# Another split of the first weight's load, and expert results collected at four points per unit, in a one-core MoE residual kernel

## The chip, the core and the metric

The kernel runs on one core of one Trainium2 chip. The metric is device time in microseconds (us), the median of the runs. All data are float32.

## What is computed

```python
x = x + L0(x, cond)      # L0: ys = cond / sqrt(512)
                         #     d  = rsqrt((ys*ys) @ (W*W) + 1e-8)
                         #     L0 = ((x * ys) @ W) * d        (per batch row)
x = x + L1(x, cond)      # L1: shared = (silu(xf @ w1) * (xf @ w3)) @ w2
                         #     s = sigmoid([xf, cond] @ router_W); top 2 of s + bias
                         #     routed = sum of 2 gates * (gelu(xf @ W1e[e]) @ W2e[e])
                         #     L1 = (shared + routed) / 3
```

x is 4 x 1024 x 512 (4096 tokens), W is 512 x 512, w1 and w3 are 512 x 1024, and there are 8 experts with 512 hidden features each.

## The kernel before, in words

The 4096 tokens are eight blocks of 512. The work has four stages, and each engine's instructions are issued in the order in which the program writes them.

**Front (L0, lines 191 to 491).** W is the tile `w0t`, 128 partitions by four chunks k of 512 columns; the product of a block sums over the four chunks. `load_w0` (L188) loads chunk by chunk: one DMA for each k, four of 256 KB, from SP's queue, behind the small load of `cond` (L191). From ACT's queue the first half of block 0 of x is loaded (L178, four DMAs, one per quarter g of 32 partitions). While these come, TensorE runs five matmuls on zeros (`WARM`, L203) and then turns `cond` (four transposes, L233), from which VectorE makes the scales `ysT` (L234, L235) and their squares (L237). Then, for each chunk k: VectorE scales the chunk into `wm` (`modulate`, L266) and turns a quarter of x (`turn_x`, L278), and ACT squares the chunk (`w0sq`, L285). On ACT's queue, behind the square of chunk 1 and of chunk 2, two loads each of the second half of block 0 are issued, and behind the square of chunk 3 the four loads of block 1. TensorE runs the products of block 0's first half chunk by chunk (L439, 16 products of 256 columns), then the norms (L313), then the second half with the rest of the norm inside (L326, L331). VectorE turns block 1 of x *before* it works out the norm (L338 to L346) and the residual sums of block 0 (L350). Block 1's products need the PSUM banks that those sums read. SP loads block 3 as soon as block 0's buffer is free.

**Shared experts, six blocks**, then **34 slots of 256 gathered tokens each** plus a number of further slots that a `Switch` takes from the data (`Slot`, weights fetched per slot, results `yr` written to DRAM as `ys_d`, L873).

**Tail: the shared experts of the last two blocks**, eight units (`Shared`, L673), called U0 to U7 below, four per block. A unit does two hidden chunks by one level of Strassen's method. On TensorE its order is: product 1 and product 2 (`begin`), products 6 and 7 in turn, product 5, the output product of the unit before (`second(0)`, L774), product 3, `second(1)`, product 4. Products 1, 6, 5, 3 go to two `ch` banks, products 2, 7, 4 to two `ot` banks (all four banks of the pool, so the next unit needs the same ones). ACT copies partial sums out of `ch` (L730) and does the SiLU (L754, L755, L764). VectorE adds `ot` to them (L734, three pairs: `add(LO, 0, LO)`, `add(HI, 1, HI)`, `add(HI, 1, LO)`) and multiplies (L756, L757 for the first chunk, L765 for the second). The last pair, `add(HI, 1, LO)`, follows product 4, and the next unit's product 2 cannot start before it, since it writes the same banks.

Beside this the tail collects the routed results, token tile by token tile (32 tiles of 128 tokens). `gather_picks(t)` fetches the tile's row from DRAM (SP, L668), copies two address columns (VectorE, L890) and issues two indirect DMAs of 256 KB from `ys_d` (GpSimd, L891) into one of ten places. `add_picks(t)` adds both with their gates (VectorE, L901, two instructions) and, for the 24 tiles of the first six blocks, writes the tile out (SP, L903). The eight tiles of the last two blocks are held until their own block's sum is added (L787) and written (L791).

When this happens is set by the list `tasks` (L941 to L977): two points per unit, one behind L757 (`task(2 * self.at)`, L758) and one behind L765 (L766). The 32 tiles are spread over 12 of the 16 points, the held eight first; a tile is added two points after its gather. Two other jobs sit in this list: `turn_last` (L922, four transposes, in U1 behind L757) and `token_sums` (L403, in U2 behind L765). Four instructions L787 lie in U4 between L757 and `add(HI, 1, LO)`.

Of the kernel before, what the change touches and what calls it, by code (L numbers as in the profile page):

```python
# [32 lines left out]
P = 128  # L33
Q = 32
# [5 lines left out]
TAIL = 2  # L40
WARM = 5
# [3 lines left out]
def kernel(  # L45
# [14 lines left out]
    nc = tc.nc  # L60
    B, S, D = x.shape
    HS = w1.shape[1]
    E, _, HE = w1e.shape
    N = B * S
    KC = D // P
    NB = N // TB
    NS = TB // P
    NT = N // P
# [11 lines left out]
    early = NB - TAIL  # L80
# [17 lines left out]
    def bank_b(name):  # L98
        return ps_b.tile([P, TB], FP, tag="b", name=name)
# [58 lines left out]
    w0_sb = w0t.rearrange("p (k d) -> p k d", k=KC)  # L158
# [12 lines left out]
    HU, KH, TH = HSC // 2, KC // 2, TB // 2  # L171

    def new_seg(blk):
        segs[blk] = seg3[:, ts((blk + 1) % 3, SEG)].rearrange("p (q c) -> p q c", c=P)

    def load_segments_part(eng, blk, lo, n, g):
        v = x_f[ds(blk * TB + lo, n)].rearrange("(q i) (g c) -> g i q c", i=Q, c=P)
        eng.dma_start(out=segs[blk][ts(g, Q), ds(lo // Q, n // Q)], in_=v[g])  # L178
# [3 lines left out]
        for g in range(KC):  # L182
            load_segments_part(eng, blk, 0, TB, g)

    def load_w0(eng, k):

        v = w0.rearrange("(g k j) o -> k g j o", g=KC, k=KC)
        eng.dma_start(out=w0_sb[:, k, :], in_=v[k])  # L188


    nc.sync.dma_start(out=cond_sb, in_=cond)  # L191
    new_seg(0)
    for k in range(KC):
        load_w0(nc.sync, k)
    for g in range(KC):
        load_segments_part(nc.scalar, 0, 0, HALF, g)


    idle = x1T6[:, 0, :]
    nc.vector.memset(idle, 0.0)  # L200
    pz = bank_b("pz")
    for _ in range(WARM):
        nc.tensor.matmul(pz, lhsT=idle[:, :P], rhs=idle, start=True, stop=True)  # L203
    nc.scalar.activation(newt, idle[:, : KC * B], AF.Square)

# [2 lines left out]
        out=ident4, in_=ident4, compare_op=ALU.not_equal, fill=1.0, base=0, pattern=[[-1, B]], channel_multiplier=1  # L208
# [4 lines left out]
    for k in range(KC):  # L213
        nc.gpsimd.affine_select(
            out=fold[ts(k, Q)],
            in_=fold[ts(k, Q)],
# [14 lines left out]
    pc = bank_b("pc")  # L231
    for k in range(KC):
        nc.tensor.transpose(pc[:, ds(k * B, B)], cond_p[:, k], ident4)  # L233
    nc.vector.tensor_copy(condT, pc[:, : KC * B].rearrange("p (k b) -> p k b", b=B))  # L234
    nc.vector.tensor_scalar(ysT, condT, scale, None, ALU.mult)  # L235
    nc.vector.memset(ys2, 0.0)
# [6 lines left out]
        out=before, in_=before, compare_op=ALU.is_ge, fill=1.0, base=0, pattern=[[-1, P]], channel_multiplier=1  # L243
# [154 lines left out]
    def token_sums(blk):  # L398
        b = x1T[blk]
        k1, k2 = slice(0, KH), slice(KH, KC)  # L400
        v = t_tiles[blk % 2].rearrange("p (n k t) -> p n k t", n=3, k=KH)
        t1, t2, t4 = (v[:, n] for n in range(3))
        sub = lambda o, i0, i1: nc.vector.tensor_tensor(o, i0, i1, ALU.subtract)  # L403
        sub(t1, b[:, k1, HI], b[:, k1, LO])
        sub(t2, b[:, k2, HI], t1)
        sub(b[:, k1, HI], b[:, k2, HI], b[:, k1, HI])
        sub(t4, b[:, k2, LO], t2)
        t_of[blk] = (t1, t2, b[:, k1, HI], t4)
# [252 lines left out]
    def segment_index(lo, hi):  # L661
        nc.vector.tensor_scalar(toks[:, lo:hi], later["toks_raw"][:, lo:hi], float(KC), part, ALU.mult, ALU.add)

    held = {}

    def fetch_row(t, rows_d):
        held[t] = row_tile(f"row{t}")
        nc.sync.dma_start(out=held[t], in_=rows_d[ts(t, P)])  # L668
# [4 lines left out]
    class Shared:  # L673
# [62 lines left out]
        def rest(self, prev, task):  # L736
            g, h = self.c = [t.rearrange("p (m t) -> p m t", m=2) for t in (later["g"], later["h"][self.at % 2])]
            self.h = h
            self.evict(0, LO)
            for i in range(2):  # L740
                self.product(self.chain[i][:, LO], i, 6, False)
                if not self.seven:
                    self.product(self.other[i][:, HI], i, 7, True)
            self.add(LO, 0, LO)
            self.evict(1, LO)
            for i in range(2):
                self.product(self.chain[i][:, LO], i, 5, False)
            self.evict(1, HI)
            if prev is not None:
                prev.second(0)  # L750
            self.add(HI, 1, HI)
            for i in range(2):
                self.product(self.chain[i][:, LO], i, 3, False)
            nc.scalar.activation(g[:, 0, HI], self.chain[0][:, LO], AF.Silu)  # L754
            nc.scalar.activation(g[:, 0, LO], g[:, 0, LO], AF.Silu)  # L755
            nc.vector.tensor_tensor(h[:, 0, HI], g[:, 0, HI], self.chain[1][:, LO], ALU.mult)  # L756
            nc.vector.tensor_tensor(h[:, 0, LO], g[:, 0, LO], h[:, 0, LO], ALU.mult)  # L757
            task(2 * self.at)  # L758
            if prev is not None:
                prev.second(1)  # L760
            for i in range(2):
                self.product(self.other[i][:, HI], i, 4, False)
            self.add(HI, 1, LO)
            nc.scalar.activation(g[:, 1, :], g[:, 1, :], AF.Silu)  # L764
            nc.vector.tensor_tensor(h[:, 1, :], g[:, 1, :], h[:, 1, :], ALU.mult)  # L765
            task(2 * self.at + 1)  # L766

        def second(self, m):
            blk, u = self.blk, self.u
            hc = 2 * u + m  # L770
            if hc == 0:
                self.py[blk] = [bank_b(f"ps{blk}_{s}") for s in range(NS)]
            for s in range(NS):
                nc.tensor.matmul(  # L774
                    self.py[blk][s],
                    lhsT=self.h[:, m, ts(s, P)],
                    rhs=w2_sb[:, hc, :],
                    start=(hc == 0),
                    stop=(hc == HSC - 1),
                )  # L780
            if blk < early and HSC - 1 > hc >= HSC - 1 - NS:
                fetch_row(blk * NS + hc - (HSC - 1 - NS), x1_d)
            if hc == HSC - 1:
                for s in range(NS):
                    t = blk * NS + s
                    r = held.pop(t)
                    nc.vector.scalar_tensor_tensor(r, self.py[blk][s], third, r, ALU.mult, ALU.add)  # L787
                    if blk < early:
                        nc.scalar.dma_start(out=base_d[ts(t, P)], in_=r)
                    else:  # L790
                        nc.sync.dma_start(out=out_f[ts(t, P)], in_=r)  # L791
# [90 lines left out]
    def gather_picks(t):  # L882

        fetch_row(t, base_d if t < early * NS else x1_d)
        spot = len(order) % 10 * 2
        order.append(t)
        picks[t] = [big[1 + (spot + i) // KC][:, (spot + i) % KC, :] for i in range(2)]
        for i in range(2):
            at = later["addr"][i][:, t : t + 1]
            nc.vector.tensor_copy(at, idx[i][:, t : t + 1])  # L890
            nc.gpsimd.indirect_dma_start(  # L891
                out=picks[t][i],
                out_offset=None,
                in_=ys_d,
                in_offset=bass.IndirectOffsetOnAxis(ap=at.bitcast(U32), axis=0),
                bounds_check=ROWS - 1,
            )

    def add_picks(t):
        for i, y in enumerate(picks.pop(t)):  # L900
            nc.vector.scalar_tensor_tensor(held[t], y, gate[i][:, t : t + 1], held[t], ALU.mult, ALU.add)  # L901
        if t < early * NS:
            nc.sync.dma_start(out=out_f[ts(t, P)], in_=held.pop(t))  # L903
# [22 lines left out]
    late = len(units)  # L926
# [4 lines left out]
    tasks = {i: [] for i in range(2 * len(units))}  # L931
# [37 lines left out]
        tasks[7 + i].append(lambda i=i: scatter(2 * i, 2))  # L969
    for blk in range(1, early):  # L970
        tasks[2 * blk * HU - 3].append(lambda blk=blk: token_sums(blk))
    span = 2 * TAIL * HU - 4
    mine = [early * NS + i for i in range(TAIL * NS)] + list(range(early * NS))
    for i, t in enumerate(mine):
        u = 2 * late + i * span // len(mine)
        tasks[u].append(lambda t=t: gather_picks(t))
        tasks[u + 2].append(lambda t=t: add_picks(t))  # L977

    for s in range(NS):
        fold_logits(NB - 2, s)  # L980
# [7 lines left out]
    for u, unit in enumerate(units):  # L988
        if u == late:
            for n in tc.Switch(later["spare"], E):  # L990
                prev.end = SURE + n
                last = prev
                for j in range(SURE, SURE + n):
                    slot = Slot(j)
                    slot.at, slot.end = prev.at + 1 + j - SURE, SURE + n
                    slot.begin()
                    slot.rest(last, lambda i: None)
                    last = slot
                last.second(0)
                last.second(1)  # L1000
            prev = None
        if u > 0:
            unit.begin()
        if u == late:
            unit.sevens()
        unit.rest(prev, run_tasks)
        prev = unit
# [41 lines left out]
```

## Time and profile before

| | |
|---|---|
| median of 3 runs | 1243.74 us (1243.33 to 1243.89) |
| the profiled execution | 1241.12 us, its span 1239.3 us |
| TensorE matmul busy | 1217.4 us (98%), mean granted clock 0.997 |
| VectorE, ACT, GpSimd busy | 414.6 us, 172.7 us, 425.3 us |
| first product of x (L439) | 12.35 us from the span's start |
| first product of block 1 | 33.90 us |
| tail, U0 to U7 and the last sums | from 1074 us to the end |
| one undisturbed unit of the tail | 18.95 us |

Times inside the profiled execution count from the start of its span.

### The profile page before, as it was taken

To read this page: it belongs to the slowest core of one execution; us is meant where nothing else is said; L and a number is where in the kernel's file an instruction comes from. 1 tells how busy PE (TensorE), PEld (TensorE's weight loads), DVE (VectorE), ACT (ScalarE), POOL (GpSimd) and SP (SyncE) were. 2 spreads that over 40 slices of the span, in tenths; PEclk is the share of its full clock that TensorE was granted. 3 is DMA by queue.
4 is the path that set the end of the run, shared out by engine and by line. 5 is a ranking of instruction groups with operands and counts; after the bars stand their busy time and mean duration, and the time that the engine had idled before them with its cause. 6 is when DMAs were issued, how large, how long until landed. Compare 5 with 4: busy or idle time off the path is not lost.

```text
span 1239.3 us, 13133 instructions
## 1 busy us (share of the span) xinstructions
PE 1217.4 (98%) x4394; PEld 818.3 (66%) x4394; DVE 414.6 (33%) x958; ACT 172.7 (14%) x379; POOL 425.3 (34%) x448
## 2 busy tenths in 40 slices
PE   8999999999999999999999999999999999989998
PEld 5444576777767767767666666666666666667665
DVE  3537565422232332222212211221122121146763
ACT  1000031211111112112100000000000000111111
POOL 3000000343430121202465566556655660046550
PEclk9999999999999999999999999999999999999999
DMA  6599413201103041310488888888878885356881
GB/s 133 107 224 218 93 35 92 53 0 35 35 1 107 26 155 58 85 51 18 126 206 220 228 230 232 217 234 235 232 216 233 236 224 170 128 179 188 292 309 68
DMA packets 120894, 183.80 MB, mean 148 GB/s; under 512 B 15060, under 2 KB 50004, under 8 KB 120808
## 3 DMA queue, kind: packets, MB, share of 16 engines
q1 hardware_dynamic: 82696, 116.58, 35.5%
q0 software_dynamic: 16448, 35.26, 11.0%
q10 hardware_dynamic: 21664, 30.94, 7.8%
q8 instruction: 38, 0.62, 0.3%
q14 instruction: 48, 0.39, 0.2%
HBM read 138.09 MB, written 44.64 MB: 147 GB/s over the span
## 4 chain that ended last, share of the span: by engine, by line
PE 92%; DMA 3%; DVE 2%; issue 1%; another core or an unknown queue 0%; SPq 0%; ACTq 0%; ACT 0%; DVEq 0%
PE ph L844 18%; PE py L868 18%; PE ch L703 17%; PE ps L774 17%; PE ot L703 13%; PE pl L439 8%; DMA w0t<-in_L_cond_weight_dram 1%; PE pq L368 1%; DMA big<-in_L_cond_W1e_dram 1%; DMA seg<-in_x_dram 1%; DVE row L901 0%; DMA ys_d<-yr 0%; PE pr L384 0%; DMA xsegs<-x_d 0%
## 5 line engine op out<-in xcount | busy, mean ns | idle before, releaser
L814 POOL DMA_INDIRECT xsegs<-x_d,toks x280 | 285.1, 1018 | 367.2 <-issue 128.1
L868 PE MATMUL py<-big,h 128*128 128x512 f32 x544 | 238.8, 592 | 0.0
L774 PE MATMUL ps<-w_sb,h 128*128 128x512 f32 x512 | 229.8, 592 | 0.0
L868 PEld LDWEIGHTS py<-big,h 128*128 128x128 f32 x544 | 103.4, 190 | 116.0 <-issue 114.3
L872 DVE COPY yr<-py 128x512 f32<-128x512 f32 x68 | 46.9, 691 | 367.4 <-issue 207.9
L644 POOL DMA_INDIRECT tok_d<-token,addr x64 | 63.5, 992 | 294.3 <-DVE addr L634 276.0
L774 PEld LDWEIGHTS ps<-w_sb,h 128*128 128x128 f32 x512 | 97.3, 190 | 96.0 <-issue 92.6
L439 PE MATMUL pl<-xT,wm 128*128 128x512 f32 (+1 forms) x288 | 118.8, 561 | 5.9 <-DVE xT L278 4.6
L844 PE MATMUL ph<-xg,big 128*128 128x256 f32 x544 | 120.3, 379 | 1.1 <-DMA big<-in_L_cond_W1e_dram 1.1
L844 PE MATMUL ph<-t,big 128*128 128x256 f32 x544 | 120.2, 379 | 0.0
L844 PEld LDWEIGHTS ph<-xg,big 128*128 128x128 f32 x544 | 103.3, 190 | 22.3 <-issue 9.1
L844 PEld LDWEIGHTS ph<-t,big 128*128 128x128 f32 x544 | 103.4, 190 | 21.3 <-issue 8.1
L703 PE MATMUL ot<-big,w_sb 128*128 128x256 f32 x448 | 110.4, 379 | 1.4 <-DVE row L787 1.4
L891 POOL DMA_INDIRECT big<-ys_d,addr x64 | 67.3, 1052 | 111.8 <-DMA row<-x_d 63.4
L851 ACT ACTIVATE h<-ph 128x512 f32<-128x512 f32 x68 | 40.6, 597 | 421.3 <-PE ph L844 252.2
L703 PEld LDWEIGHTS ot<-big,w_sb 128*128 128x128 f32 x448 | 85.0, 190 | 14.1 <-DVE row L787 1.8
L734 DVE TENSOR_TENSOR g<-ot,g 128x256 f32<-128x256 f32 x96 | 40.6, 423 | 155.0 <-PE ot L703 103.9
L439 PEld LDWEIGHTS pl<-xT,wm 128*128 128x128 f32 x288 | 53.5, 194 | 57.4 <-issue 46.3
L703 PE MATMUL ch<-w0t,seg 128*128 128x256 f32 x256 | 62.7, 380 | 2.6 <-issue 2.5
L703 PE MATMUL ch<-t,seg 128*128 128x256 f32 x256 | 63.1, 379 | 0.0
L734 DVE TENSOR_TENSOR h<-ot,h 128x256 f32<-128x256 f32 x96 | 40.6, 423 | 62.1 <-PE ot L703 39.0
L756 DVE TENSOR_TENSOR h<-g,ch 128x256 f32<-128x256 f32 x32 | 13.5, 421 | 134.5 <-PE ch L703 109.4
(163 smaller groups left out, 945.6 us busy)
## 6 DMA issues: line engine op xcount, KB each, us to landing
big<-in_L_cond_W1e_dram SPq DMA_DIRECT2D x136, 256.0 KB
big<-in_L_cond_W2e_dram SPq DMA_DIRECT2D x34, 1024.0 KB
ys_d<-yr ACTq DMA_DIRECT2D x68, 256.0 KB
x_d<-back SPq DMA_DIRECT2D x32, 256.0 KB
row<-x_d SPq DMA_DIRECT2D x32, 256.0 KB
out_dram<-row SPq DMA_DIRECT2D x32, 256.0 KB
base_d<-row ACTq DMA_DIRECT2D x24, 256.0 KB
row<-base_d SPq DMA_DIRECT2D x24, 256.0 KB
```

Of the source, the lines that this page charges most:

```text
L439: nc.tensor.matmul(pas[oc][:, ds(lo, n)], lhsT=wms[b][:, k, oc, :], rhs=xTs[blk][:, k, ds(lo, n)], start=(k == 0), stop=(k == KC - 1),)
L644: ins = nc.gpsimd.indirect_dma_start(out=tok_d, out_offset=bass.IndirectOffsetOnAxis(ap=later["addr"][i][:, t : t + 1].bitcast(U32), axis= ...
L703: nc.tensor.matmul(out, lhsT=lhs[:, k, :], rhs=rhs[:, k, :], start=start and k == 0, stop=k == KH - 1, skip_group_check=not start,)
L734: nc.vector.tensor_tensor(c[:, m, cols], p[:, half], c[:, m, cols], ALU.add)
L756: nc.vector.tensor_tensor(h[:, 0, HI], g[:, 0, HI], self.chain[1][:, LO], ALU.mult)
L774: nc.tensor.matmul(self.py[blk][s], lhsT=self.h[:, m, ts(s, P)], rhs=w2_sb[:, hc, :], start=(hc == 0), stop=(hc == HSC - 1),)
L814: nc.gpsimd.indirect_dma_start(out=seg[:, q, :], out_offset=None, in_=x1_segs, in_offset=bass.IndirectOffsetOnAxis(ap=toks[:, c : c + 1].b ...
L844: nc.tensor.matmul(ph[:, i], lhsT=weights[j][0][:, k, ts(hp * per + i, P)], rhs=xg[j][:, k, :], start=(k == 0), stop=(k == KC - 1),)
L851: nc.scalar.activation(self.h[:, ts(hp, per), :], ph, AF.Gelu)
L868: nc.tensor.matmul(py, lhsT=self.h[:, hc, ts(s, P)], rhs=weights[j][1][:, hc, :], start=(hc == 0), stop=(hc == HC - 1))
L872: nc.vector.tensor_copy(r, py)
L891: nc.gpsimd.indirect_dma_start(out=picks[t][i], out_offset=None, in_=ys_d, in_offset=bass.IndirectOffsetOnAxis(ap=at.bitcast(U32), axis=0) ...
```

## The change

Two places are edited.

In the front, W comes in eight DMAs instead of four: first chunk 0 alone, in four parts of 32 partitions (64 KB each), then, for each quarter of 32 partitions, its chunks 1 to 3 in one DMA (192 KB each). All are still issued from SP. The second batch stands behind the loads of x in the program, which go through ACT's queue. Of the five matmuls on zeros, two stay ahead of the transposes of `cond`, and three run behind them.

In the tail, a list `pumps` with a counter `passed` replaces `tasks` for the picks. `pump()` is called four times per unit: behind `add(LO, 0, LO)` (point 0), behind `add(HI, 1, HI)` (point 1), behind L757 and the unit's first task (point 2), and at the end behind its second task (point 3): 32 points in all. Tile i of the list is gathered at point 25 i / 32, rounded down, and added six points later, ahead of that point's gathers. The list is in another order: the four tiles of block 6, twelve early ones, the four of block 7, the other twelve. `turn_last`, `reload_last` and `token_sums` stay in `tasks`.

```diff
-    def load_w0(eng, k):
-        v = w0.rearrange("(g k j) o -> k g j o", g=KC, k=KC)
-        eng.dma_start(out=w0_sb[:, k, :], in_=v[k])
+    def load_w0(eng, g, lo, hi):
+        v = w0.rearrange("(g k j) o -> g j k o", g=KC, k=KC)
+        eng.dma_start(out=w0_sb[ts(g, Q), lo:hi, :], in_=v[g][:, lo:hi, :])
...
-    for k in range(KC):
-        load_w0(nc.sync, k)
+    for g in range(KC):
+        load_w0(nc.sync, g, 0, 1)
     for g in range(KC):
         load_segments_part(nc.scalar, 0, 0, HALF, g)
+    for g in range(KC):
+        load_w0(nc.sync, g, 1, KC)
...
-    for _ in range(WARM):
+    for _ in range(WARM // 2):
         nc.tensor.matmul(pz, lhsT=idle[:, :P], rhs=idle, start=True, stop=True)
...
     for k in range(KC):
         nc.tensor.transpose(pc[:, ds(k * B, B)], cond_p[:, k], ident4)
+    for _ in range(WARM - WARM // 2):
+        nc.tensor.matmul(pz, lhsT=idle[:, :P], rhs=idle, start=True, stop=True)
...
+    pumps, passed = {}, []
+    def pump():
+        if not passed:
+            return
+        for work in pumps.get(passed[0], []):
+            work()
+        passed[0] += 1
...
             self.add(LO, 0, LO)
+            pump()
...
             self.add(HI, 1, HI)
+            pump()
...
             task(2 * self.at)
+            pump()
...
             task(2 * self.at + 1)
+            pump()
...
-    span = 2 * TAIL * HU - 4
-    mine = [early * NS + i for i in range(TAIL * NS)] + list(range(early * NS))
+    mine = list(range(early * NS))
+    mine = [early * NS + i for i in range(NS)] + mine[: len(mine) // 2] + list(range(NT - NS, NT)) + mine[len(mine) // 2 :]
+    points = 4 * TAIL * HU
     for i, t in enumerate(mine):
-        u = 2 * late + i * span // len(mine)
-        tasks[u].append(lambda t=t: gather_picks(t))
-        tasks[u + 2].append(lambda t=t: add_picks(t))
+        p = i * (points - 7) // len(mine)
+        pumps.setdefault(p, []).append(lambda t=t: gather_picks(t))
+        pumps.setdefault(p + 6, []).insert(0, lambda t=t: add_picks(t))
...
         if u == late:
+            passed.append(0)
             unit.sevens()
```

## Prediction

> **What bounds the kernel now.** I read the page's first part, the chain of work for the front, a table of 1 us stretches of the front, the waits of TensorE, and the timeline of the tail. The page says that only TensorE matters:
>
> ```profile
> PE 1217.4 (98%) x4394; PEld 818.3 (66%) x4394; DVE 414.6 (33%) x958; ACT 172.7 (14%) x379; POOL 425.3 (34%) x448
> ```
>
> So the change is worth what it takes from the stretches in which TensorE waits. The chain of the first 45 us (start, length, what) shows the first of them:
>
> ```profile
> 3.09 16.73 DMA w0t<-in_L_cond_weight_dram
> ...
> 19.84 0.33 ACT w0sq L285
> ...
> 20.20 0.51 ACTq L178
> ...
> 21.29 6.34 DMA seg<-in_x_dram
> ...
> 27.71 2.49 DVE xT L278 x4
> ...
> 33.90 3.70 PE pl L439 x8
> ```
>
> The reader is to see a relay: W's last chunk lands at 19.8 us, only then does ACT issue block 1 of x, which lands at 27.63 and is turned by VectorE, and 6.2 us after its start (33.90 - 27.71) TensorE begins block 1. The table of the same time has, per stretch, its length, the busy shares, the granted clock, the share of the 16 DMA engines and GB/s:
>
> ```profile
> 10.00:11.00 1.00, 0.00 (x0) 0.00 (x0) 0.15 (x1) 0.00 (x0) 0.93 (x3) 1.00 0.28 93
> 14.00:15.00 1.00, 1.00 (x4) 0.82 (x3) 0.00 (x0) 0.00 (x0) 0.00 (x0) 0.50 0.88 222
> 19.00:20.00 1.00, 0.48 (x3) 0.08 (x1) 0.16 (x1) 0.16 (x1) 0.00 (x0) 1.00 0.26 65
> 24.00:25.00 1.00, 1.00 (x6) 0.90 (x5) 0.00 (x0) 0.47 (x1) 0.00 (x0) 1.00 1.19 197
> ```
>
> While W alone loads, a quarter of the DMA engines is busy (0.26 to 0.28). When x comes along (14 us, and from 21 us on) the share is 0.88 and more. So W is slow because it sits on about four engines, not because memory is.
>
> In the tail TensorE waits twice (us in total, times, longest):
>
> ```profile
> PE ot L703 <- DVE g L734: 5.3, 1, 5.3
> PE ot L703 <- DVE row L787: 1.4, 1, 1.4
> ```
>
> The timeline of U1 (start, busy, engine, line) shows why:
>
> ```profile
> 1103.79 1.89 PE L703 MATMUL ot<-w0t,w_sb 128*128 128x256 f32 x8
> 1104.77 0.42 DVE L757 TENSOR_TENSOR h<-g,h 128x256 f32<-128x256 f32 x1
> 1105.26 2.49 DVE L922 STREAM_TRANSPOSE big<-xsegs 128x512 f32<-128x512 f32 x4
> 1107.68 4.40 DVE L901 SCALAR_TENSOR_TENSOR row<-big,gate,row 128x512 f32<-128x512 f32 x6
> 1111.99 0.33 DVE L890 COPY addr<-idx 128x1 int32<-128x1 int32 x4
> 1112.23 0.41 DVE L734 TENSOR_TENSOR g<-ot,g 128x256 f32<-128x256 f32 x1
> 1112.70 3.66 PE L703 MATMUL ot<-x1T,w_sb 128*128 128x256 f32 x8 [5.30 <-DVE g L734]
> ```
>
> Product 4 starts at 1103.79. Behind L757 VectorE does `turn_last`, three tiles' adds and address copies, and only then the pair that frees the banks. How much it may do there comes from an undisturbed unit, U7: L757 ends 2.41 us before product 4 starts (1223.95 against 1226.36), and TensorE needs the banks 3.46 us after it (1207.40 to 1210.86 in U6), with 0.47 us from the add's start to the matmul (1112.23 to 1112.70). Room without a stall: 2.41 + 3.46 - 0.47 = 5.4 us. In U1 it did 7.2 us of work and also started 3.8 us late: L754 began 5.0 us behind product 3's start (1098.63 to 1103.64) where U2 has 1.07. I can't see what held ACT there; GpSimd was in its first run of twelve gathers, the only thing special to that stretch.
>
> **What the skill says.** (1) "DMA: Bandwidth & Descriptors", section "Why a DMA increments its semaphore by 16 and not by 1": a DMA issued from SP or ACT uses the largest number of engines, up to 16, that divides the outermost dimension (of size over 1) of both its sides. Before, W's source has outermost g = 4 and its target 128 partitions: four engines. The measured 0.26 to 0.28 of 16 agrees. After, both sides lead with 32: sixteen, as do the loads of x, which show 0.88. (2) "TensorE: Matmul & The Clock Gate", section "Part 1: The HAM clock gate (the "warmup" mystery)": about 3.4 us without work halve TensorE's clock, about 3.4 us of work restore it. The trace agrees: after 3.35 us idle before 12.35 the clock column falls to 0.50 from 14 to 17 us; the first pass on zeros starts every 0.85 us until 6.76, then every 0.43.
>
> **Part 1: the load of W.** Removed: four DMAs on four engines. Added: eight on sixteen. By 5.0 us the old front had moved some 0.43 MB (the table's stretches up to there, summed), slowed by the router's small packets. cond, W and half of block 0 are 1.6 MB, so 1.15 MB remain; at 197 to 222 GB/s (rows above) that takes 5.2 to 5.9 us. The built program makes the second batch wait for earlier loads (the first part of x, the first part of chunk 0, the second part of x, the second part of chunk 0), since completion semaphores are reused after eight DMAs; as the cond load takes 2.1 us from issue to use (0.76 to 2.88), I add 0.5 us for that gap. Chunks 1 to 3 then land together at about 11 us (bounds 9.5 and 13) instead of 19.84. SP has nothing else queued; its next load, block 3, waits for VectorE.
>
> **From there, two paths.** VectorE needs 0.49 + 0.45 us per chunk, so the products of chunk 1 start at 12.0; twelve products at 0.435 us (16 of double width take 13.93 in the chain) end at 17.2, against 22.66 before. From there to the end of block 0 TensorE took 10 us (22.66 to 32.6): 27.2. The other path: ACT's three squares and the four loads of the second half between them come bunched: two issues are 0.82 us, so block 1's first issue is at 11 + 1.65 = 12.65. Before, landing came 7.43 us behind it (20.20 to 27.63); now the second half's 0.5 MB is still in flight, and block 3 starts sooner too, so I add 0.8: 20.9, and 6.2 later TensorE starts block 1: 27.1. The paths meet: 27.2 instead of 33.90, **6.7 us won**. Bounds: 8.5 with the landing at 9.5 (TensorE's own path then decides), 4.5 at 13. Behind it TensorE is dense until 1039 us, so the gain arrives whole.
>
> **Part 2: the matmuls on zeros.** The same five; nothing added. Two end at 4.9 us, the transposes follow (cond is there at 3.4), `ysT` is ready by 6 instead of 9.4, and three more fill the time to about 9, when chunk 0 and half of x should be ready. Cost nothing while chunk 0 is the later one. If the clock count restarts at the transposes, they end at 10.5 and the first four products move 1.7 us, of which the wait for chunk 1 hides 1.2. If they hid nothing: 1.7.
>
> **Part 3: the picks.** Counts stay: 64 gathers, 64 adds, 64 copies, 32 rows, 24 writes. Only places change. In U1 behind L757 now stand `turn_last` (2.42), two tiles' adds (2.95, from the row of four in other units, 2.98) and two copies (0.22): 5.6 us against 5.4 of room, a stall of 0.25. With ACT late again as before (3.8) it is 4.05. I take half the delay, since the twelve gathers in a row become two to four per point: 2.15, both ends kept. In U4, point 2 holds one tile (1.5 + 0.2) ahead of the four L787, which end with their banks: its 1.35 us go. So 6.65 becomes 2.15: **4.5 us won**, bounds 6.4 and 2.6. In the other units point 2 holds one or two tiles, at most 3.2 us of 5.4: hidden. Point 0 delays `add(HI, 1, HI)` by up to 3.2 us, and product 4 needs that pair only 8 us later (9.2 to 17.2 of the unit): hidden. Point 3 ends before the next unit's first pair (1.4 + 3.2 of 5.45). On SP three row loads now stand ahead of `reload_last`: some 2 us, with 20 to spare before U1's `turn_last`. GpSimd gets 1.28 tiles per 4.74 us, 3.4 us at 1.32 a gather: fits. An add comes six points, 28 us, behind its gather (19 before). The last add moves from U6 into U7's point 2, about 9 us before the last sums: hidden.
>
> **Sum.** 6.7 + 4.5 = 11.2 us from the profiled 1241.12 (span 1239.3 plus 1.8): 1229.9. The median of the runs is 2.6 above the profiled one; I take the difference over: 1243.74 - 11.2 = **1232.5 us**.
>
> **Rivals.** (a) *Block 1's load becomes the late one.* It stays chained behind ACT's squares, and three loads now overlap (second half, block 1, block 3). For: DMA is saturated from 22 to 33 us (1.2). Against: it carries the same bytes as before. If it lands at 24.5, the front wins 3.2: 1243.74 - 7.7 = 1236.0. (b) *The tail's stall stays*: ACT late again and another pair late, tail won 0 to 2.6: 1235.7 on the middle. For: nothing I know causes the delay. Against: the load behind L757 is 1.6 us smaller. (c) *W still comes on few engines.* Then chunks 1 to 3 land together at 19.8 and all twelve products follow: TensorE ends the half at 19.8 + 0.95 + 5.2 = 26 instead of 22.66: 3.3 lost, 4.5 won: 1242.5. Against it: x's loads in the same form. (d) *Slower: VectorE stands in a point on a gather that has not landed.* The tail moves 33.6 MB (sum of its stretches). From the first gather at 1080 to the last add's place some 150 us pass, so it decides below 224 GB/s. The stretch of gathers alone ran at 203 GB/s: 33.6 MB then take 165 us, 15 us of waiting against 6.7 won: 1252. Against: 305 to 333 GB/s once rows and gathers mix.
>
> **Chances.** Forecast 0.64, (a) 0.14, (b) 0.14, (c) 0.04, (d) 0.04. A measurement here tells 0.2% (2.5 us) from no change. Faster: 0.92, same: 0.04 (c), slower: 0.04 (d). Range 1228.5 to 1238: the best ends (8.5 + 6.4 = 14.9, 1228.8) down to rivals (a) and (b) with two us beside them; (c) and (d) are left out.
>
> **What would show it.** W's last landing near 11 us with a DMA share over 0.8 before it; first product near 9; no half clock from 14 to 17; block 1's first product near 27; in U1 a stall of 0.3 to 4 and none in U4. A landing of W past 15 us, or a new wait on L901 or on a gather, would prove it wrong.

## The result, and the profile after

| | before | after |
|---|---|---|
| median | 1243.61 us (4 runs, 1243.33 to 1243.89) | 1235.63 us (4 runs, 1233.46 to 1236.83) |
| the profiled execution | 1241.12 us, span 1239.3 | 1235.95 us, span 1234.2 |
| chunks 1 to 3 of W landed | 19.82 us (the last chunk) | 10.53 us |
| first product of x | 12.35 us | 8.93 us |
| first product of block 1 | 33.90 us | 28.08 us |
| first product of the tail to the end of the span | 165.2 us | 163.1 us |

The ratio is 0.9934 with an interval of 0.9917 to 0.9951: 8.2 us less, from 6.1 to 10.3. 11.2 us less were forecast. The time lies inside the range, and the faster side was the likely one; but two of the sum's terms are smaller than forecast, and the two profiles show only 5.2 us between them. Where the rest stands took the experiments.

First the line of busy times in the page of after, against that of before:

```profile
PE 1217.8 (99%) x4394; PEld 817.6 (66%) x4394; DVE 414.1 (34%) x958; ACT 172.6 (14%) x379; POOL 427.5 (35%) x448
```

TensorE's 4394 matmuls are the same and as long. What was won is waiting time alone. The chain of work of the front (start, length, what):

```profile
4.85 5.68 DMA w0t<-in_L_cond_weight_dram
...
11.54 4.04 DMA seg<-in_x_dram
...
15.60 6.17 DMA seg<-in_x_dram
...
21.89 2.49 DVE xT L282 x4
...
28.08 3.70 PE pl L443 x8
```

The relay is still there, with W's 16.7 us cut to 5.7. Now a load of x is behind W, and block 1 of x behind that. Two stretches of the front that answer to those of before (length, busy shares of PE, PEld, DVE, ACT and POOL, granted clock, share of the DMA engines, GB/s):

```profile
8.00:9.00 1.00, 1.00 (x4) 0.45 (x3) 0.00 (x0) 0.00 (x0) 0.93 (x7) 1.00 1.12 217
14.00:15.00 1.00, 1.00 (x6) 0.87 (x6) 0.00 (x0) 0.00 (x0) 0.00 (x0) 1.00 0.85 225
```

While W loads, all DMA engines are busy (1.12, where 0.28 stood), and at 14 us TensorE has its full clock, where it had half. From 1030 us on, W1e's load ahead of the tail included, TensorE's waits are (us in total, times, longest):

```profile
PE ch L717 <- ACT g L744: 2.7, 2, 2.3
PE ph L862 <- DMA big<-in_L_cond_W1e_dram: 1.6, 1, 1.6
PE ch L717 <- issue: 1.2, 1, 1.2
```

Both waits of before, 5.3 in U1 and 1.4 in U4, are gone. But new ones stand at L717, ahead of `ch`: 0.40 us in U0 (at 1076.86) and 3.85 at the start of U1 (1.25, 2.35, and 0.25 for `h` in a line not shown). The timeline (start, busy, engine, line, operation, in brackets the idle time before it) has the two long ones:

```profile
1085.81 0.38 ACT L744 ACTIVATE g<-ch 128x256 f32<-128x256 f32 x1 [1.20 <-PE ch L717]
...
1090.02 0.38 ACT L744 ACTIVATE h<-ch 128x256 f32<-128x256 f32 x1 [3.83 <-PE ot L717]
1090.46 1.13 PE L717 MATMUL ch<-w0t,seg 128*128 128x256 f32 x4 [1.25 <-issue]
...
1094.36 0.38 ACT L744 ACTIVATE g<-ch 128x256 f32<-128x256 f32 x1 [3.96 <-remote]
1094.80 1.23 PE L717 MATMUL ch<-w0t,seg 128*128 128x256 f32 x4 [2.35 <-ACT g L744]
...
1095.85 0.42 DVE L748 TENSOR_TENSOR g<-ot,g 128x256 f32<-128x256 f32 x1 [10.28 <-remote]
...
1104.89 2.49 DVE L940 STREAM_TRANSPOSE big<-xsegs 128x512 f32<-128x512 f32 x4
1107.22 1.89 PE L717 MATMUL ot<-w0t,w_sb 128*128 128x256 f32 x8
1107.30 2.95 DVE L919 SCALAR_TENSOR_TENSOR row<-big,gate,row 128x512 f32<-128x512 f32 x4
...
1110.29 0.41 DVE L748 TENSOR_TENSOR g<-ot,g 128x256 f32<-128x256 f32 x1
```

The reader is to see two things. The lower part is what the change was to do: around product 4 (1107.22) VectorE does `turn_last` and two tiles' adds, and the pair comes at 1110.29, in time: TensorE does not wait for it. The upper part is the lateness of ACT and VectorE that the profile of before had in the same unit, here ending some 5 us earlier in the unit. VectorE does nothing for 10.28 us and ACT makes only three evictions in that time.

What they wait for is a count of TensorE. When a product is done, TensorE raises a semaphore, a counter that ACT and VectorE wait for, and the packed trace holds the times at which it rose. The products whose last matmuls end at 1085.76, 1088.35 and 1089.21 by the trace are counted only at 1090.00, 1094.34 and 1095.76, so 4.2 to 6.6 us later, and the two evictions and VectorE's add above start 0.02 to 0.09 us behind these counts. In the profile of before, product 3's first bank ends at 1099.65 and is counted at 1103.61; this is what held ACT there. The ends of matmuls are modelled in a trace, so it cannot tell a late product from a late count; the matmuls behind these products start at their usual pace. "Late" and "lateness" below mean this.

Here it stops TensorE directly, and TensorE's clock is halved behind it:

```profile
1092.00:1096.00 4.00, 1.65 (x7) 0.73 (x5) 0.15 (x1) 0.54 (x2) 1.85 (x2) 0.96 1.04 388
1096.00:1100.00 4.00, 3.75 (x9) 2.37 (x9) 1.61 (x8) 0.88 (x3) 2.45 (x3) 0.61 0.44 136
```

Comparing the matmuls' starts in order, the gain of the profiled pair runs so: 5.8 us at block 1, 4.0 from 184 us on (at 180.9 us after has 3.41 us at half clock behind a wait of 2.5 us that both kernels have), 3.7 from 317 (a late copy of ACT), 3.0 from 1037 (W1e's wait is 1.6 instead of 1.1, and the matmuls behind it), 2.7 from 1077, below zero at U1's start, 3.6 once before has had its own stall in U1, 5.1 behind U4.

The runs came in sets at different times, and the kernel before took 1243.6, 1243.1, 1236.5, 1242.1 and 1235.9 us in them, so times are compared within a set only.

### The profile page after: what moved, and what is told of

The parts are those of the page before. It is cut to its first block, busy times and chain, and to the rows that moved or that the text cites. A ratio compares the mean times of both kernels' runs of the same rounds, so it can differ in the third digit from the quotient of the medians.

```text
span 1234.2 us, 13140 instructions
## 1 busy us (share of the span) xinstructions
PE 1217.8 (99%) x4394; PEld 817.6 (66%) x4394; DVE 414.1 (34%) x958; ACT 172.6 (14%) x379; POOL 427.5 (35%) x448
## 4 chain that ended last, share of the span: by engine, by line
PE 95%; DMA 3%; DVE 1%; another core or an unknown queue 0%; issue 0%; SPq 0%; ACT 0%; ACTq 0%; DVEq 0%
PE ph L862 18%; PE py L886 18%; PE ps L792 18%; PE ch L717 18%; PE ot L717 13%; PE pl L443 8%; DMA seg<-in_x_dram 1%; DMA big<-in_L_cond_W1e_dram 1%; PE pq L372 1%; DMA w0t<-in_L_cond_weight_dram 0%; PE pr L388 0%; DMA row<-x_d 0%; DVE xT L282 0%; DMA ys_d<-yr 0%
## 5 line engine op out<-in xcount | busy, mean ns | idle before, releaser
L717 PE MATMUL ot<-big,w_sb 128*128 128x256 f32 x448 | 110.9, 381 | 0.0
L717 PEld LDWEIGHTS ot<-big,w_sb 128*128 128x128 f32 x448 | 85.2, 190 | 12.4 <-issue 0.8
L717 PE MATMUL ch<-w0t,seg 128*128 128x256 f32 x256 | 65.7, 392 | 7.0 <-issue 3.8
L717 PE MATMUL ch<-t,seg 128*128 128x256 f32 x256 | 63.1, 379 | 0.0
L717 PEld LDWEIGHTS ch<-w0t,seg 128*128 128x128 f32 x256 | 49.5, 196 | 16.4 <-issue 4.6
```

Of the source, the lines that this page charges most:

```text
L717: nc.tensor.matmul(out, lhsT=lhs[:, k, :], rhs=rhs[:, k, :], start=start and k == 0, stop=k == KH - 1, skip_group_check=not start,)
```

## The experiments

My theory from these two profiles: the front's gain is real and somewhat smaller than forecast, since block 1 of x lands late; the tail's is what VectorE's shorter work behind L757 frees, and the lateness is not shortened at all, it only falls elsewhere. Rivals: the new places of the picks cause the lateness that after shows; the lateness comes from the first gathers or from the start of the tail, and can be moved out; the front's gain is lost again behind it.

### One part alone: front, tail, load

`e1_front` is the kernel before with the whole front of the change; `e3_load` the same with all zeros ahead of the transposes, as before (shown against `e1_front`):

```diff
-    for _ in range(WARM // 2):
+    for _ in range(WARM):
...
-    for _ in range(WARM - WARM // 2):
-        nc.tensor.matmul(pz, lhsT=idle[:, :P], rhs=idle, start=True, stop=True)
```

`e2_tail` is the kernel before with the tail's part alone:

```diff
+            pump()
...
-        tasks[u].append(lambda t=t: gather_picks(t))
-        tasks[u + 2].append(lambda t=t: add_picks(t))
+        pumps.setdefault(p, []).append(lambda t=t: gather_picks(t))
+        pumps.setdefault(p + 6, []).insert(0, lambda t=t: add_picks(t))
```

> The front's edits alone (the load of W and the split of the matmuls on zeros), the tail as before. Theory (the two edits are independent, and the front's gain of 5.8 us at block 1's first product is carried to the end, less what TensorE loses to its clock on the way): block 1's first product at 28.1 us, the time 4 to 6 us under the kernel before. Rival (most of the gain is eaten on the way, as 1.7 us of half clock near 181 us and 0.6 us at a weight load in the changed kernel's profile suggest): 2 to 4 us under it. Whatever is lost must show in the difference of the matmuls' start times.

> The tail's edit alone (picks at four points per unit), the front as before. Theory: the stalls of the old tail (5.3 us, 1.4 us, and half clock after the first) go, and a wait for ACT and VectorE at the start of U1 comes in: net 2 us won, block 1's first product at 33.9 us. Rival 1 (the wait in U1 is chance and the profile happened to show it): up to 6 us won. Rival 2 (edits need each other): 0 or a loss.

> The front's load alone, all five matmuls on zeros ahead of the transposes as before, the tail as before. Theory (the split of the zeros is nearly free, since the scales are then ready at 9.7 us and chunk 0 has its product at about 10.5, still ahead of chunk 1 at 11.5): block 1's first product within 0.5 us of that with the split (28.1), the time the same within 0.5 us. Rival (the split keeps the clock up, or the late first product pushes the rest back): 1 to 2 us slower than with the split.

Measured in one set, with the kernel before at 1243.06: `e1_front` 1238.52, ratio 0.9959 (0.9943 to 0.9975), 5.1 us less; `e3_load` 1238.46, 0.9966 (0.9954 to 0.9978), 4.2 less; `e2_tail` 1240.52, 0.998 (0.9972 to 0.9987), 2.5 less (1.6 to 3.5). Front and tail sum to 7.6, and the change measured 8.2 with 6.1 to 10.3 in its own set: within these intervals the parts add up, and neither is seen to hide the other. Splitting the zeros is worth nothing that these runs can tell. `e1_front` and `e3_load` keep before's stalls in the tail (5.3 and 1.3 us, 5.2 and 1.3 us in their waits of TensorE). `e2_tail` has neither, but 3.9 us ahead of `ch` in U1, as after has. So the front is worth its 4 to 5 us, and the tail 2.5 and not 4.5.

### The gathers later

The lateness fell into the first run of twelve gathers in both profiles, so `e4_late` starts them six points later in the changed kernel:

```diff
-        p = i * (points - 7) // len(mine)
+        p = 6 + i * (points - 12) // len(mine)
...
-        pumps.setdefault(p + 6, []).insert(0, lambda t=t: add_picks(t))
+        pumps.setdefault(p + 5, []).insert(0, lambda t=t: add_picks(t))
```

> The changed kernel with the first gather at point 6 instead of 0 (20 points for the 32 tiles, added five points later). It tells what holds ACT and VectorE at the start of U1 (4 us each, TensorE waits some 4.2 us). Theory A (the first run of twelve gathers, back to back on GpSimd, holds them): the delay moves with the gathers, out of 1086 to 1096 us, or goes. Theory B (it belongs to the place in the code or to the time behind the Switch, such as a late instruction fetch): the delay stays at 1086 to 1096 us, with no gather there. If it goes and nothing new comes, the time is 3 to 4 us under the changed kernel; under B it is the same within 1 us.

Measured: 1240.91, ratio 0.9978 (0.9967 to 0.9989) to the kernel before. That is some 5 us worse than the changed kernel's ratio, from another set. U1 is clean, and the lateness has moved with the gathers. Their first run now lasts from 1101.2 to 1119.4 us, in U2; ACT's SiLU behind it has stood for 8.15 us, where a unit without lateness has 3.91. TensorE loses only 0.68 us there. It comes again in the second run (1130.1 to 1151.7), where it stops TensorE for 3.09 and 1.75 us, and at the end of the third (1157.4 to 1171.1), for 0.72. The timeline of `e4_late`:

```profile
1121.32 0.38 ACT L770 ACTIVATE g<-ch 128x256 f32<-128x256 f32 x1 [8.15 <-PE ot L717]
...
1150.53 0.38 ACT L744 ACTIVATE g<-ch 128x256 f32<-128x256 f32 x1 [5.41 <-remote]
...
1150.97 1.13 PE L717 MATMUL ch<-t,seg 128*128 128x256 f32 x4 [3.09 <-issue]
...
1153.42 0.42 DVE L748 TENSOR_TENSOR g<-ot,g 128x256 f32<-128x256 f32 x1 [9.61 <-PE ch L717]
```

So it does not belong to the start of the tail. It goes with the gathers, as theory A said, and starting them later only moved it to where it cost as much. The other profiles agree: wherever a count of the tail's units is over 1 us late, it is so within a long run of gathers or just behind it, and the lateness ends within 2 us of the run's last gather (1102.6 and 1104.3 us in before, 1094.2 and 1095.9 in after). But not every long run has it: in the second run of twelve in before (1151.2 to 1167.8) ACT's SiLU, at 1163.8, has waited its usual 3.91 us. And the order could be the other way about, since a run also ends when VectorE, while it stands, copies no more addresses.

### What the lateness hangs on

Four kernels in one set. `e5_shift` adds 64 one-element operations to ACT and 64 to VectorE in an early block; `e6_nogather` leaves out the gathers, and with them the routed experts' sum; `e7_direct` loads adjacent rows instead of gathered ones, so that the wrong rows are added; `e8_again` is the changed kernel unaltered.

```diff
...
+    def pad():
+        for _ in range(8):
+            nc.vector.memset(dummy[0], 0.0)
+            nc.scalar.activation(dummy[1], dummy[1], AF.Copy)
...
+    for i in range(8):
+        tasks[2 * (2 * HU + i) + 1].append(pad)
```

```diff
-            nc.gpsimd.indirect_dma_start(
-                out=picks[t][i],
...
-            )
+            nc.gpsimd.dma_start(out=picks[t][i], in_=ys_d[ds((2 * t + i) * P, P)])
```

> The changed kernel with 64 one-element operations more on ScalarE and 64 more on VectorE, eight at a time in eight tasks of the second shared block, far ahead of the tail: they cost at most a few us of those two engines in a stretch where TensorE is dense, and they move the instructions of the tail against the blocks in which an engine's instructions are fetched. Theory F (an engine runs out of instructions in the tail, since a fetch waits behind the gathers' traffic): the delay of ScalarE and VectorE at 1090 to 1096 us (waits of 3.8, 4.0 and 10.3 us with TensorE's 1.25 and 2.35 us behind them) leaves its place, by a unit or more, and the time changes by 2 us or more in either direction. Theory G (it is the load of the gathers' and rows' transfers that delays them): same place within 3 us, time within 1 us of the changed kernel's, 1235 to 1236.

> The changed kernel without the 64 gathers of the picks in the last two blocks: the address copies, the adds and the rows' transfers stay, the adds read what the buffers held. It leaves the routed experts' sum out of the output. Theory G (gathers delay ScalarE and VectorE): no wait of ScalarE or VectorE of 3 us or more that no producer explains in the tail, no wait of TensorE there over 1 us, and the tail from its first product to the end 3 to 6 us shorter than the changed kernel's 163.1 us, so 1230 to 1232.5 us. Theory F (instruction fetches land late whatever loads the queues) or another cause in the order of the work: the delay at U1's start stays, and the time is within 1.5 us of 1235.6.

> The changed kernel with each gather of 128 rows of 2 KB replaced by a plain transfer of 128 adjacent rows of the same size, from the same queue at the same place: the same bytes, no list of addresses and no 1.3 us of GpSimd for each. The rows added are not the picked ones. If the bytes on the DMA engines delay ScalarE and VectorE, the delay of 3 to 10 us at the start of U1 stays (perhaps earlier, since nothing paces the transfers to one in 1.3 us) and the time is 1234 to 1237. If GpSimd's making of the gathers' lists does it, the delay goes as without gathers: 1230 to 1232.5 us.

> The changed kernel once more, unaltered, with a second profile. If the place of the delay belongs to the program (theories F and G both say so), ScalarE and VectorE wait again at 1090 to 1096 us within 2 us, and TensorE's waits of 1.25 and 2.35 us stand there again; time 1234 to 1237. If it belongs to the execution, the delay stands elsewhere or is of another length by more than 2 us.

Measured, with the kernel before at 1236.53 in this set: `e5_shift` 1228.92 (ratio 0.9936, 0.9923 to 0.995), `e6_nogather` 1227.68 (0.9921, 0.9906 to 0.9937), `e7_direct` 1230.68 (0.9942, 0.9927 to 0.9957), `e8_again` 1228.96 (0.9942, 0.9927 to 0.9958). The set was about 6.5 us faster for before and after alike, and the surprise is `e8_again`: the same program, without the lateness. Its U1, from the timeline and the table of stretches:

```profile
1085.04 0.42 DVE L748 TENSOR_TENSOR g<-ot,g 128x256 f32<-128x256 f32 x1 [3.75 <-PE ot L717]
...
1094.48 2.49 DVE L940 STREAM_TRANSPOSE big<-xsegs 128x512 f32<-128x512 f32 x4
...
1096.89 2.95 DVE L919 SCALAR_TENSOR_TENSOR row<-big,gate,row 128x512 f32<-128x512 f32 x4
...
1099.88 0.42 DVE L748 TENSOR_TENSOR g<-ot,g 128x256 f32<-128x256 f32 x1
...
1100.36 1.99 PE L717 MATMUL ot<-x1T,w_sb 128*128 128x256 f32 x8
```

```profile
1084.00:1088.00 4.00, 4.00 (x20) 3.52 (x19) 0.99 (x5) 1.15 (x3) 3.09 (x4) 1.00 1.04 387
1088.00:1092.00 4.00, 4.00 (x12) 2.03 (x11) 0.94 (x4) 0.38 (x1) 3.08 (x4) 1.00 1.04 389
```

GpSimd makes gathers at the same pace (3.08 of 4 us), the DMA engines are as full (1.04) and move as much (389 GB/s) as in after's stretches of the lateness (1.04, 388), and TensorE does not wait. In `e8_again` sixteen gathers follow each other (1074.2 to 1095.3 us), and every count of TensorE comes within 0.12 us of the end of a product, up to the last sums. So neither the program nor its load on the queues is enough for the lateness; it takes something of the execution. Both theories that my expectation weighed said that the place belongs to the program: both fall in that form. Late fetches of instructions are not needed to explain it, since ACT and VectorE start as soon as TensorE's count has risen.

Two things on record bear on that something. The chip alone does not decide it: the set at 1243.1, with the lateness, and this one ran on the same chip. And the traces differ long before the tail: those with the lateness hold 507 to 531 rises of TensorE's count, where 635 or 636 matmuls raise it, with the first losses between 200 and 250 us; those without hold all. Whether the loss of records and the lateness have one cause, or whether the recording itself delays the counts, these runs do not tell.

From the tail's first product to the end of the span the profiles give:

| profile | tail, us | late ACT and VectorE |
|---|---|---|
| before | 165.2 | yes |
| `e1_front`, `e3_load` | 165.6, 164.9 | yes |
| `e2_tail`, after | 163.5, 163.1 | yes |
| `e4_late` | 167.2 | yes, in U2, U4 and U5 |
| `e8_again`, `e5_shift` | 156.9, 157.0 | no |
| `e6_nogather` | 156.9 | no |
| `e7_direct` | 162.5 | no, but a wait of 4.2 us for another reason |

The lateness costs after 6.2 us (163.1 - 156.9): 3.85 us of waits at U1's start and 1.7 us of half clock make 5.55 of it. And without it the gathers cost nothing on the path: 156.9 with all 64 and with none (their adds and address copies stand in both).

`e7_direct` went as neither theory said. Without the 1.3 us per gather on GpSimd the plain transfers come all at once, `turn_last` waits 4.38 us for the DMA queues, and TensorE stands 4.23 us for the pair behind it. That is not a test of the lateness, which the set lacked. It suggests that GpSimd's slow pace spares the reload of block 7; one profile has it.

### The kernel before again, and a better front

`e9_before` is the kernel before, unaltered. `e10_sqrt` is the changed kernel with ACT's table for Sqrt loaded ahead of time; `e11_three` is that with W's last three chunks in two steps.

```diff
         nc.scalar.activation(norm_part, pn, AF.Copy)
+        nc.scalar.activation(newt[:, :B], idle[:, :B], AF.Sqrt)
```

```diff
-    for g in range(KC):
-        load_w0(nc.sync, g, 1, KC)
+    for lo, hi in ((1, 2), (2, KC)):
+        for g in range(KC):
+            load_w0(nc.sync, g, lo, hi)
```

> The kernel before once more, unaltered, with a second profile. In the kernel's first profile TensorE stood 5.3 us for ScalarE in the second unit of the tail, after ScalarE and VectorE had started late by 3.8 us or more; the repeated changed kernel's profile had no such lateness. Theory X (the lateness came with the first profile's execution, not with the program): here the stall in U1 is 0.5 to 3 us, U4's of 1.35 us is still there, and the tail from its first product to the end lasts 158 to 161 us against the 165.2 us of the first profile, 1.5 to 3.5 us over the changed kernel's undisturbed tail. Theory Y (the program's own order of gathers and reload makes it): 5.3 us again within 0.7, the tail 163 to 166 us, and the tail's part of the change's gain is 6 us or more where nothing disturbs it.

> The changed kernel with a Sqrt of four columns on ScalarE right after the eviction of the norm's partial sums, so that the table of 1.28 us is loaded at 19 us where ScalarE is idle, and not at 24.3 us between the variance and its root. VectorE's chain to the first modulated product then starts 1.3 us earlier, and TensorE's wait of 1.0 us ahead of block 1's first product (at 27.9 us) should go whole: first product at 26.9 to 27.0 us, and 1.0 us less in all against the changed kernel. If something else holds that product (the transposes of block 1, landing at 21.6 us), it stays at 27.9 and the time is the changed kernel's.

> As the run before it, and W's last three chunks of a quarter are loaded as chunk 1 alone and then chunks 2 and 3 together, so in eight transfers. If the wait of 1.46 us ahead of chunk 1's products (10.1 to 11.6 us) comes from chunk 1 being bound to chunks 2 and 3, the products of chunk 1 start at 9.5 to 10.2 us and up to 1.4 us more is won, if chunk 2 is there by 12.2 us. If issuing four more transfers of 0.4 us each on SP, or the 64 KB pieces, makes the last chunk land later than 12.5 us, it is won nowhere: 0 to 1 us slower than the run before it.

Measured, with the runs of the kernel before at 1242.13: `e9_before` 1240.4 (0.9989, 0.9977 to 1.0002, the same kernel), `e10_sqrt` 1232.92 (0.9927, 0.9908 to 0.9947), `e11_three` 1232.89 (0.9923, 0.9903 to 0.9943). All three profiles have the lateness again.

`e9_before` decides less than I wanted: the lateness is there, smaller. Its U1:

```profile
1099.54 1.89 PE L703 MATMUL ch<-x1T,seg 128*128 128x256 f32 x8
...
1103.74 0.42 DVE L756 TENSOR_TENSOR h<-g,ch 128x256 f32<-128x256 f32 x1 [4.94 <-remote]
...
1112.01 1.99 PE L703 MATMUL ot<-x1T,w_sb 128*128 128x256 f32 x8 [3.69 <-DVE g L734]
```

L756 comes 4.2 us behind product 3's start (1099.54 to 1103.74), where the same line of `e8_again`, its L772, has 2.0 (1091.65 to 1093.65): 2.2 us late, as the count is (1101.43 by the trace, counted at 1103.65), with a stall of 3.7. The first profile was 3.8 late with 5.3. The stall without the lateness is then 1.5 in both (3.7 - 2.2, 5.3 - 3.8). Theory X had named 0.5 to 3 us and a tail of 158 to 161, theory Y 4.6 us or more and 163 to 166; 3.7 and 161.9 lie between them. What the two profiles agree on is that the stall follows the lateness one for one, on top of some 1.5 us that belong to the program.

`e10_sqrt` did as expected: in after and `e8_again` ACT's two-step root (a table load of 1.28 us and then 0.21 us of work) stood between the variance and the first modulated product, with TensorE waiting 1.0 to 1.2 us for it. Now the table is loaded at 18.68, while ACT is idle:

```profile
18.68 1.28 ACT L326 ACT_TABLE_LOAD   x1
...
24.53 0.22 ACT L344 ACTIVATE newt<-var 128x16 f32<-128x16 f32 x1 [4.35 <-DVE var L343]
```

Block 1's first product starts at 26.79 instead of 27.88 (`e8_again`) or 28.08 (after), and TensorE goes through without a wait. The Trainium skill, page "ScalarE: Activation LUTs", section "What ACT_TABLE_LOAD costs", gives 1283 ns for the load, as measured here. It adds about 1380 ns of drain per switch; no such time shows here: in `e8_again` the root starts 0.02 us behind the load (25.62 against 24.32 + 1.28), and the load 0.07 us behind the variance that it waits for.

`e11_three` took the other wait in the front (of 1.3 us ahead of chunk 1's products 0.2 are left, ahead of chunk 2's), but block 1's first product came only 0.35 us sooner, at 26.44: block 1 of x landed at 21.45 and VectorE's chain behind it is now the last, as its 0.6 us of waiting on `big` shows. Its time is that of `e10_sqrt`. Both have lower ratios than the changed kernel's 0.9934, but the intervals overlap: the profiles show that block 1 starts 1.1 to 1.3 us sooner in `e10_sqrt`; that the whole kernel is faster by as much is not shown.

### Without gathers, once more

The same kernel as `e6_nogather`, to be run in a set with the lateness:

> The changed kernel without the 64 gathers of the last two blocks once more (it leaves the routed experts' sum out of the output). Four profiles taken together, the earlier one of this kernel among them, had no lateness of ScalarE and VectorE in the tail at all, with the kernel before at 1236.5 us; in the other sets of executions every profile had it, with the kernel before at 1242 to 1243.6 us. If the kernel before stands at 1240 or more here, the lateness is to be expected, and the profile tells: no wait of ScalarE or VectorE over 3 us without a producer means that the gathers' transfers are needed for it (theory G), and the time is 1228 to 1231; waits of 4 to 10 us with no producer at the start of the second unit mean that the gathers are not needed and that it hangs on something else that comes there, such as the landing of the engines' own instructions (theory F), and the time is 1232 to 1236. If the kernel before stands at 1236 to 1237, it tells nothing new.

The kernel before stood at 1235.88, so this set had no lateness to show: 1228.56 (0.9933, 0.9919 to 0.9947), tail 157.1. Inconclusive. Counting all profiles, nine had the lateness, in sets where before took 1242 us or more, and five had none, in sets where it took 1236.5 or less. Each kernel has one profile in a set, so whether every execution of a set is alike isn't known: in the set at 1242.1 one run of before took 1237.12. That a kernel without gathers would be spared in the former sets isn't known either. What makes TensorE's counts late stays open.

## Why the prediction was right, and where it was not

- **W's load.** Right. Landing at 10.53 (predicted 11), DMA share over 1 (over 0.8), first product at 8.93 (near 9), chunk 1's products at 11.55 (12.0), end of the half at 16.9 (17.2), no half clock at 14 us. Rival (c), W on few engines, is out.
- **The two paths that meet at 27.2.** The mechanism was right, one term mis-sized. TensorE's own path ends at 26.9 (28.08 - 1.19 of wait). The other path lands block 1 of x at 21.77, not 20.9; behind it come the 6.2 us as predicted. The forecast took 7.43 us from block 1's first issue to its landing before; but 20.20 is its second issue, the first stands at 19.85, so it was 7.8. After the change it is 9.2 (12.55 to 21.77): the overlap of the loads costs 1.4 us, not 0.8. The chain shows part of it. The last of the block's four loads is issued only at 15.60, when a load of block 0's second half has landed, the kind of wait that the prediction counted for W's second batch and left out here. It isn't all: in `e4_late` and `e11_three` that issue comes at 14.23 and 13.76, and the block lands at 21.9 and 21.45 all the same. So 5.8 us were won, not 6.7. This is rival (a) in a mild form. One pair of profiles says 5.8; in the eight profiles of the changed front block 1 starts between 27.32 and 28.68, and in the three of the front before between 32.81 and 33.90. (The bounds of 8.5 and 4.5 come out of the prediction's own sums as 8.2 and 4.7.) I had taken the 6.2 us as one piece; inside it stood the 1.28 us of table load that `e10_sqrt` took out.
- **"TensorE is dense until 1039 us, so the gain arrives whole."** Wrong in the profiled pair: 2.8 of the 5.8 us were gone by 1037. 1.7 us are a half clock behind a wait of 2.5 us at 177 us that both kernels have. The wait stands in the profile of before too (2.53 us, ahead of 185.35), and "dense" passed over it. It isn't the change's doing: of the fourteen profiles, eight have 3.41 us at half clock there and six have none, `e9_before` with and `e8_again` without. 0.6 us go at the wait for W1e (1.1 in before, 1.6 in after, none in `e8_again`) and the matmuls behind it.
- **The zeros.** Cost nothing, as said: `e3_load` against `e1_front`.
- **U4.** Right: the 1.35 us went.
- **U1's stall.** The arithmetic of the room was right and the term for the delay failed. With 5.6 us of work against 5.4 of room a stall of 0.25 was forecast without lateness; `e8_again` has U2's product 1 at 1098.54 and its product 2 at 1100.36, and 1.73 us between such starts in U1 of after (1083.87 to 1085.60): 0.1. The failed step is "I take half the delay, since the twelve gathers in a row become two to four per point". The twelve gathers in a row came all the same (1078.44 to 1094.16), since U0's points stand close together (the addresses are copied at 1077.51, 1081.37, 1083.40 and 1085.25). The lateness came with them, not halved but up to 6.6 us long, and at a place where it stops TensorE at once. What held ACT, which the prediction could not see, was TensorE's own late count. In the sets without it, the kernel before is some 6.5 us faster and the changed kernel too (1235.6 to 1229.0): it seems to add the same to both and to cancel. What the change takes from U1 is then about 1.5 - 0.1, and with U4's 1.35 the tail wins 2.8 us. `e2_tail` measured 2.5 (1.6 to 3.5), the profiled pair 2.1. That the lateness costs the two kernels alike is read from times of different sets; no profile of the kernel before without it was had.
- **Rivals.** (b), the stall stays with ACT late again, is the one that came: the tail won 2.5, within its 0 to 2.6. That its 1235.7 us is nearly what was measured (1235.6) is luck: it adds 6.7 in the front and 1.3 in the tail, where the parts measured 5.1 and 2.5. Its "another pair late" is the pair at U1's start. The other side's (d), waits on gathers, did not come: no wait on L919 or on a gather stands in TensorE's way.

Summed up by parts: 5.8 in the front and 2.8 in the tail are 8.6, and 8.2 (6.1 to 10.3) were measured. 11.2 were forecast; 0.9 of the difference is block 1's landing and 1.7 the lateness taken as half gone.

## What to carry to other kernels

A wait in one profile that no engine's work explains may belong to that execution: look up in the trace when the count that it waited for rose, profile the kernel twice, and forecast the change without the wait before its removal is priced. A transfer is made quicker by spreading it over the DMA engines only until the next one in the relay is last, so walk the whole chain behind it for what it holds, a table load among it. Room for VectorE, counted between the point where banks are freed and the point where they are needed, predicted U1's stall to 0.2 us where the counts came in time (0.25 forecast, 0.1 found).

## What the runs showed of the hardware

- The same program, with the same matmuls, the same pace of gathers and as full DMA engines (388 and 389 GB/s), has TensorE's products counted up to 6.6 us late in some executions and within 0.12 us in others (after and `e8_again`). In the nine profiles that have it, it falls in long runs of gathers and ends within 2 us of their last; ACT and VectorE, which wait for the count, stand for up to 10.3 us. The cause is open.
- A wait of 2.53 us of TensorE was followed by 3.41 us at half clock in eight profiles of fourteen. The Trainium skill, page "TensorE: Matmul & The Clock Gate", section "Part 1: The HAM clock gate (the "warmup" mystery)", says that the clock is judged in windows of 3413 ns that run freely; the 3.41 us and the chance of it agree. It asks for about 3.4 us without work; here 2.53 us were enough. The wait is 2.53 us in before, after and `e8_again` alike, and of these only after has the half clock behind it.
- Gathers of 128 rows of 2 KB followed each other every 1.32 us on GpSimd (1.02 and 0.30 between), and 64 of them cost nothing beside TensorE where its counts came in time (156.9 us of tail with and without).
